# A 7x7 depthwise convolution cut image by image into tiles of six by four pixels, with each projection behind its own image's attention

## The chip, the core and the metric

The kernel runs on one core of a Trainium2 chip. The number that counts is the device time of one execution in microseconds: the median of three runs, which is 3268.41 us for the kernel before (3267.57 to 3269.32). One more execution was taken with the hardware profiler on. All data is float32. A core has a matrix engine (PE, with its weight loads shown apart as PEld), a vector engine (DVE), a scalar engine (ACT), GpSimd (POOL), and the sync engine (SP), which here only issues transfers between device memory and on-chip memory.

## The reference

The input is four images of 256 channels by 64 x 64 pixels. Two residual layers follow one another; each one normalises its input over groups of 8 channels first.

```python
# layer 0: 8 heads of 32; keys and values from a 2x2 strided convolution (1024 of each per image)
x = x + softmax((q k + q pos) * scale) v
# layer 1: 4 areas of 16 rows per image, attention inside an area (1024 keys), 8 heads of 32
qkv = conv1x1(gn(x), w_qkv)
out = softmax(q k * scale) v                       # per area
out = out + depthwise_conv7x7(v_full, w_pe, b_pe)  # over the whole image, zero padding 3
x = x + conv1x1(out, w_proj)
```

The change is about the line with `depthwise_conv7x7`: each of the 256 channels of v, in each of the four images, is convolved with its own 7 x 7 taps, and the sum with the attention's output goes through the last 1 x 1 product (`w_proj`), called the projection below.

## The kernel before, in words

**Units and steps.** The whole program is one line of 128 units, written out by hand: 64 for layer 0 (A), 16 per image, then 64 for layer 1 (B), 16 per image. A unit is the attention of 512 queries and four heads over 1024 keys, in 8 steps of 128 keys. In each step `scores` makes four products q k (line 261, tile `s`), ACT takes their exponentials (line 265, tile `p`), `weighted` makes four products with v (line 272, tile `av`), and DVE adds up the exponentials for the divisors (line 797). Once a unit, `divisors` makes four products with ones (line 281).

**Side work.** Everything else is planned with `at(unit, step, what)` and woven into the steps. Products go into a queue of tasks (`task`, `soon_tasks`, `advance`): a step makes the next part of the first task (two or three parts if many wait), and all of them write one on-chip accumulator tile, `ps_side`, which exists once. The helper `product` (line 155) makes four matmuls of 32 output channels each. Side work is q, k and v of layer 0 (`q0ps`, `k0ps`, `v0ps`), v of layer 1 with its channels in rows (`vals_ps`), k and q of layer 1 (`k1ps`, `q1ps`), the convolution (`conv_ps`, line 732) and the projection (`ops`). The order of instructions on each engine is the order in which the Python code emits them; SP issues its transfers in that order too, and a transfer that waits holds up all later ones of SP.

**The convolution before.** `plan_values` writes v of all four images to one device array `vals` with rows of pixels outermost, and separately to `vala`, from which attention reads. When the last value of the last image is stored, `plan_conv` takes four channels at a time, for all four images together: 64 times it loads 126 partitions (42 rows of pixels, three times, each shifted by one pixel) for two halves of the image with six transfers, and for every second one three transfers of banded weights. A banded matrix product over rows does seven taps in one direction and three in the other at once, so three shifted products make the seven columns. That is 24 matmuls of 126 x 32 weights against 256 columns for each group of four channels. These run from unit 70.5, one group every 0.52 units, to about unit 104.

**The projection before.** Since the convolution of all images ends that late, the attention of images 0 to 2 is stored (`store_att`, array `attd`) and read back; projections of these images are planned from unit 105.3 on, one chunk of 512 pixels every 0.8 units (`late`, `spread`). Only image 3 projects straight behind its attention. For one chunk, `load_rest` loads the convolution (one transfer of 2 KB runs), `add_conv` adds it, the bias and the attention on DVE, and `project` makes 16 matmuls.

Of the kernel before, what the change touches and what calls it, by code (L numbers as in the profile page):

```python
# [33 lines left out]
BAND = HH // 2 + 2 * HALO  # L34
BROWS = 42
TC = 8
# [18 lines left out]
def direct_path(  # L55
# [31 lines left out]
    attd = [[dram.tile([P, CT, CH], FP, name=f"attd_{b}_{c}") for c in range(NCH)] for b in range(B - 1)]  # L87

    vals = dram.tile([HH + 2 * HALO + BROWS - BAND, C, B, XP], FP, name="vals")

    vala = [[dram.tile([4, HD, NH, 4, XP], FP, name=f"vala_{b}_{a}") for a in range(NAREA)] for b in range(B)]
    conv = dram.tile([C, B, N], FP, name="conv")

    bands = dram.tile([C // TC, 9, BROWS + HH // 2 - 1, TC], FP, name="bands")

# [368 lines left out]
    def plan_b(b, u):  # L464
# [13 lines left out]
        def make_k(a, qd, half):  # L478
# [3 lines left out]
            for t in range(CT):  # L482
# [7 lines left out]
            S.activation(  # L490
                k[:, qd, :].rearrange("p (j t i) -> p t j i", t=4, i=32)[:, 2 * half : 2 * half + 2],
                ps.rearrange("p (t j i) -> p t j i", t=2, i=32), AF.Identity, bias=bqkv_sb[:, 1, qd : qd + 1],
            )
# [3 lines left out]
        def load_v(a, half):  # L497
            vcs[a, half] = pool.tile([P, NH // 2, 4, XP], FP, tag="vc", name=f"vc_{b}_{a}_{half}", bufs=2)
            nc.sync.dma_start(
                vcs[a, half], vala[b][a][:, :, half * NH // 2 : (half + 1) * NH // 2].rearrange("t c h r x -> (t c) h r x")  # L500
            )

        def make_v(a, half):

            if half == 0:
                kvs["v"] = v_tile(("B", b, a))
            v, vc = kvs["v"], vcs.pop((a, half))
            V.transpose(
                out=v[:, :, half * P : (half + 1) * P].rearrange("p (r j) (h c) -> p h r j c", j=2, c=HD),
                in_=vc[:, :, :, HALO : HALO + WW].rearrange("p h r (j w) -> p h r j w", w=HD),  # L510
            )
            if half == 1:
                vs["B", b, a] = v
# [17 lines left out]
        for a in range(NAREA):  # L531
            g = u + 4 * a
            at(g - 6, 3, lambda a=a: load(a))
            for t in range(CT):
                at(g - 5, 2 + 3 * t, lambda a=a, t=t: norm(a, t))
            for n in range(4):
                at(g - 4, 1 + 4 * n, lambda a=a, n=n: task(2, make_k, a, n // 2, n % 2))
            for half in range(2):
                at(g - 3, 2 + 5 * half, lambda a=a, half=half: load_v(a, half))
                at(g - 2, 2 + 4 * half, lambda a=a, half=half: make_v(a, half))  # L540
# [5 lines left out]

        def store_att(c):
            nc.sync.dma_start(attd[b][c], atts.pop(("B", b, c)))
# [5 lines left out]
        def load_rest(c):  # L554
            cv = chunk_tile(f"cv_{b}_{c}")
            nc.sync.dma_start(cv, conv[:, b, c * CH : (c + 1) * CH].rearrange("(t p) n -> p t n", p=P))
            att = None
            if c == NCH - 1:
                load_residual(c)
            if b < B - 1:  # L560
                att = chunk_tile(f"at_{b}_{c}")
                nc.sync.dma_start(att, attd[b][c])
            rest[c] = cv, att

        def add_conv(c):
            cv, att = rest[c]
            if c < NCH - 1:
                load_residual(c)
            if att is None:
                att = atts["B", b, c]  # L570
            for t in range(CT):
                V.scalar_tensor_tensor(cv[:, t, :], cv[:, t, :], bpe_sb[:, t : t + 1], att[:, t, :], ALU.add, ALU.add)

        def project(c, to):
            cv, ps = rest[c][0], ps_side(f"ops_{b}_{c}_{to}")
# [7 lines left out]
            V.scalar_tensor_tensor(xm[:, to, :], ps, bproj_sb[:, to : to + 1], xm[:, to, :], ALU.add, ALU.add)  # L583
# [4 lines left out]

        for c in range(NCH):
            g, j = u + 2 * c + 3, 5  # L590
            if b < B - 1:
                at(g, j + 1, lambda c=c: store_att(c))
                g, j = 0, int(NKT * (late + spread * (b * NCH + c)))
            else:
                at(g, j, lambda c=c: add_conv(c))
                at(g, j + 2, lambda c=c: soon_tasks([(2, project, c, to) for to in range(CT)]))
                g, j = (g - 1, 5) if c < NCH - 1 else (g - 2, 2)
            at(g, j, lambda c=c: load_rest(c))
            if b < B - 1:
                at(g, j + 4, lambda c=c: add_conv(c))  # L600
                at(g, j + 6, lambda c=c: soon_tasks([(2, project, c, to) for to in range(CT)]))
# [13 lines left out]

    def plan_zeros(g):


        def zeros():
            zero = pool.tile([P, 8 * B * XP], FP, tag="rows", name="zero", bufs=2)  # L620
            V.memset(zero, 0.0)
            for lo, hi in ((0, 3), (67, 71), (71, 74)):
                nc.sync.dma_start(
                    vals[lo:hi].rearrange("r c b x -> (r c b x)").rearrange("(p n) -> p n", n=8 * B * XP),
                    zero[: (hi - lo) * C // 8],
                )
            flat = bands.rearrange("k x i c -> (k x i c)").rearrange("(p n) -> p n", p=P)
            nc.sync.dma_start(flat, zero[:, : flat.shape[1]])

        def taps():  # L630
            tap = pool.tile([NTAP, C], FP, tag="cout", name="tap", bufs=2)
            nc.sync.dma_start(tap, wpe.rearrange("c k -> k c"))
            for n in range(7):
                nc.sync.dma_start(
                    bands[:, :7, BAND - 1 - n, :].rearrange("k x c -> x k c"),
# [808 lines left out]
```

## Time and profile before

| | before |
|---|---|
| median of three runs | 3268.41 us (3267.57 to 3269.32) |
| the profiled execution: its own time, and its span | 3270.47 us, 3268.7 us |
| granted PE clock, mean | 0.997 |
| busy share PE / DVE / ACT / POOL | 98% / 76% / 77% / 15% |
| matmul records | 29730 |
| DMA packets, of them under 512 B | 319853, 182652 |
| mean DMA rate | 122 GB/s |

The span runs from the first to the last instruction of the profiled execution. Each matmul of this float32 program appears as two matmul records and two weight loads, so the 1536 matmuls of the convolution are 3072 records. "Busy" time of a group is the union of its records, which overlap, since four matmuls that use different quarters of the array run side by side. The chain that ended last is followed back from the last instruction; a stretch of it on one engine is the time in which that engine set the pace. A bracket with an arrow says what ended an idle time.

### The profile page before, as it was taken

The numbers are of one execution on the slowest core, as the hardware profiler recorded it, in microseconds if no ns is written. First come the engines' busy times: TensorE is split into PE (matmuls) and PEld (weight loads), VectorE is DVE, ScalarE is ACT, GpSimd is POOL, SyncE is SP. The second block draws the span as 40 slices with busy tenths as digits, with TensorE's granted clock in tenths as the row PEclk, the third lists the DMA queues.
The fourth block names the chain that finished last, engine by engine and source line by source line (L and its number), as shares of the span: only waits on it lengthen the run. The fifth ranks groups of instructions, "written<-read, shape, count | busy, mean of one in ns | idle before, by whom it ended". The sixth has DMA issues, their size and how long they took to land.

```text
span 3268.7 us, 72561 instructions
## 1 busy us (share of the span) xinstructions
PE 3218.2 (98%) x29730; PEld 961.1 (29%) x29730; DVE 2491.6 (76%) x2621; ACT 2525.6 (77%) x2993; POOL 487.2 (15%) x923
## 2 busy tenths in 40 slices
PE   7999999999999999999999999999999999999997
PEld 4233323333233322222222333333333322222221
DVE  3777897779877787778876767666776778888887
ACT  3888788887888888888887777777777787776765
POOL 0111121111211111111111111111111111111111
PEclk9999999999999999999999999999999999999999
DMA  5312212313322213553236667676766643445431
GB/s 179 80 64 73 77 66 90 100 59 116 100 69 84 65 63 91 148 138 113 82 120 158 162 151 178 159 174 141 180 171 153 172 142 123 166 147 172 155 121 57
DMA packets 319853, 397.27 MB, mean 122 GB/s; under 512 B 182652, under 2 KB 215708, under 8 KB 319192
## 3 DMA queue, kind: packets, MB, share of 16 engines
q1 hardware_dynamic: 291064, 356.06, 38.5%
q0 software_dynamic: 28448, 36.48, 4.2%
q8 instruction: 236, 3.87, 0.5%
q14 instruction: 105, 0.86, 0.1%
HBM read 285.98 MB, written 106.42 MB: 120 GB/s over the span
## 4 chain that ended last, share of the span: by engine, by line
PE 94%; DMA 2%; issue 1%; ACT 1%; DVE 1%; SPq 0%; POOL 0%; DVEq 0%; ACTq 0%; POOLq 0%
PE s L261 33%; PE av L272 29%; PE conv_ps L732 5%; PE den L281 4%; PE k0ps L155 3%; PE k1ps L155 3%; PE q1ps L155 3%; PE v0ps L155 3%; PE q0ps L155 3%; PE ops L155 3%; PE vals_ps L155 3%; ACT p L265 1%; DVE p L797 1%; DMA conv<-cout 0%; DMA rows<-vals 0%
## 5 line engine op out<-in xcount | busy, mean ns | idle before, releaser
L797 DVE TENSOR_TENSOR p<-p 128x1024 f32<-128x1024 f32 x1792 | 2113.3, 1219 | 623.1 <-ACT p L265 583.3
L265 ACT ACTIVATE p<-s 128x1024 f32<-128x1024 f32 x2048 | 2016.9, 1027 | 571.9 <-PE s L261 564.0
L261 PE MATMUL s<-q,k_A 32*128 32x512 f32 x4096 | 608.2, 640 | 1.4 <-ACT p L265 0.9
L261 PE MATMUL s<-q,k_B 32*128 32x512 f32 x4096 | 588.7, 640 | 1.1 <-ACT p L265 0.8
L272 PE MATMUL av<-p,v_A 128*32 128x512 f32 x4096 | 551.1, 603 | 0.0
L272 PE MATMUL av<-p,v_B 128*32 128x512 f32 x4096 | 546.0, 604 | 0.0
L308 POOL DMA_DIRECT2D rb<-recs x508 | 252.4, 502 | 454.1 <-DMA recs<-few 377.5
L306 POOL DMA_DIRECT2D recs<-few x127 | 70.2, 553 | 1423.2 <-DVE sums L305 1372.1
L261 PEld LDWEIGHTS s<-q,k_A 32*128 32x128 f32 x4096 | 176.3, 183 | 357.8 <-issue 273.3
L261 PEld LDWEIGHTS s<-q,k_B 32*128 32x128 f32 x4096 | 162.5, 182 | 363.3 <-issue 290.5
L272 PEld LDWEIGHTS av<-p,v_A 128*32 128x32 f32 x4096 | 89.4, 108 | 383.0 <-issue 335.0
L272 PEld LDWEIGHTS av<-p,v_B 128*32 128x32 f32 x4096 | 87.6, 108 | 378.8 <-issue 332.9
L732 PE MATMUL conv_ps<-rows,band 126*32 126x256 f32 x3072 | 195.1, 379 | 0.0
L732 PEld LDWEIGHTS conv_ps<-rows,band 126*32 126x32 f32 x3072 | 123.0, 139 | 113.0 <-issue 78.3
L297 POOL DMA_DIRECT2D rows<-den_sb x127 | 74.6, 587 | 433.3 <-ACT den_sb L290 424.1
L281 PE MATMUL den<-p,ones 128*32 128x512 f32 x1024 | 137.8, 605 | 0.4 <-DVE p L797 0.4
L155 PE MATMUL ops<-cv,wp_sb 128*32 128x512 f32 x1024 | 129.8, 600 | 6.0 <-issue 6.0
L155 PE MATMUL vals_ps<-hv,wqkv_sb 128*32 128x512 f32 x1024 | 130.1, 596 | 3.9 <-ACT vout L669 3.8
L155 PE MATMUL k0ps<-taps,wk_sb 128*32 128x256 f32 x2048 | 130.6, 383 | 3.0 <-ACT taps L243 3.0
L155 PE MATMUL k1ps<-h,wqkv_sb 128*32 128x512 f32 x1024 | 128.7, 593 | 2.4 <-ACT cout L739 1.6
L155 PE MATMUL q0ps<-hq,wq_sb 128*32 128x512 f32 x1024 | 129.8, 592 | 0.0
L155 PE MATMUL q1ps<-h,wqkv_sb 128*32 128x512 f32 x1024 | 129.7, 596 | 0.1
(87 smaller groups left out, 1594.9 us busy)
## 6 DMA issues: line engine op xcount, KB each, us to landing
rb<-recs POOLq DMA_DIRECT2D x508, 64.0 KB, 2.4
rows<-vals SPq DMA_DIRECT2D x128, 189.0 KB
rows<-vals SPq DMA_DIRECT2D x128, 188.8 KB
rows<-vals SPq DMA_DIRECT2D x128, 188.7 KB
vala<-vout SPq DMA_DIRECT2D x128, 144.0 KB
vals<-vout SPq DMA_DIRECT2D x256, 72.0 KB
vc<-vala SPq DMA_DIRECT2D x32, 576.0 KB
hq<-in_x SPq DMA_DIRECT2D x32, 512.0 KB
```

The source lines that it names most:

```text
L155: T.matmul(out[cols, :], lhsT=lhsT[:, cols], rhs=rhs, start=start, stop=stop)
L261: T.matmul(pairs[h // 2][:, h % 2, :], lhsT=k[rows, unit[0], j * P : (j + 1) * P], rhs=q[rows, :], start=True, stop=True,)
L265: exps = [lambda i=i: S.activation(p[i], pairs[i], AF.Exp, scale=SCALE) for i in range(2)]
L272: T.matmul(av[HD * h : HD * h + HD, :], lhsT=v[:, j, unit[0] * P + HD * h : unit[0] * P + HD * h + HD], rhs=p[h // 2][:, h % 2, :], start= ...
L281: T.matmul(dens[g][HD * h : HD * h + HD, :], lhsT=ones, rhs=p[h // 2][:, h % 2, :], start=True, stop=True,)
L297: G.dma_start(rows, den_sb[0:P:HD, :])
L306: G.dma_start(recs.rearrange("h (q n) -> (h q) n", n=CH // HD), few[:, 1, :])
L308: G.dma_start(rb[HD * h : HD * h + HD, :], recs[h : h + 1, :].to_broadcast([HD, CH]))
L732: T.matmul(ps[HD * m : HD * m + HD, i], lhsT=band_tiles[k][:, g, :, part + c], rhs=xs[:, m % 2, c, :, 3 * g : 3 * g + WW], start=(g == 0), ...
L797: soon(1, lambda i=i: V.tensor_add(ps[0][i], ps[0][i], ps[j][i]))
```

## The change

Six rows by four columns of output pixels become one tile. With its halo a tile reads 12 x 10 pixels = 120 contraction rows, and one matrix of 120 x 32 (24 pixels and 8 rows of nothing needed) makes all 49 taps in one product. An image has 11 x 16 such tiles, which are the 176 columns of the product. A channel of an image then takes one matmul.

- `plan_values`: v is stored with the four columns of a tile apart (`vals[b]`, one array per image; runs of 18 numbers), in four transfers per half chunk where there were eight per chunk; the halves get tiles of their own (`vout`, which share five buffers, tag `vc`, with the tiles that attention reads).
- `plan_zeros`: the 120 x 32 matrices are put together once, early (`matrices`, units 4 to 13.4: 16 times ten small loads and a store to `mats`).
- `plan_conv`, `load_rows`, `convolve`: per image and group of eight channels, four loads (`rows`), every second time one of matrices (`band`), eight matmuls, one copy out of `ps_side`, one store. This is 128 groups. The loads run three groups ahead.
- The times: values of images 0 to 3 start at units 17.8, 42, 54.5 and 67; convolutions at units 36, 58, 75.5 and 93.5, one group every 0.53 to 0.68 units.
- `store_att` and `attd` are gone: every image projects straight behind its attention, from `add_conv(c)` at unit u + 2c + 3 (u the image's first unit) on. Its convolution is loaded one unit before, with 16 transfers (8 rows of pixels, 2 halves of the channels) of 64-byte runs instead of one.
- Columns of a tile stand apart in `cv`, so `add_conv` and the last addition read or write with a stride (`by_column`); the keys of an area change their order to that of the values (`make_k` copies in two halves, `make_v` transposes in four parts of two heads).

The diff, cut to its core:

```diff
-BAND = HH // 2 + 2 * HALO
-BROWS = 42
-TC = 8
+TY, TX, NY, XT, NP, TC = 6, 4, 11, WW // 4 + 2, 120, 16
+BY, BX = 12 + 7, 10 + 3
...
-            S.activation(
-                k[:, qd, :].rearrange("p (j t i) -> p t j i", t=4, i=32)[:, 2 * half : 2 * half + 2],
-                ps.rearrange("p (t j i) -> p t j i", t=2, i=32), AF.Identity, bias=bqkv_sb[:, 1, qd : qd + 1],
-            )
+            for n in range(2):
+                S.activation(
+                    k[:, qd, :].rearrange("p (r g t f x) -> p t r g f x", r=4, g=2, t=4, f=2)[:, 2 * half + n],
+                    ps[:, n * 256 : (n + 1) * 256].rearrange("p (r x g f) -> p r g f x", r=4, g=2, f=2),
+                    AF.Identity, bias=bqkv_sb[:, 1, qd : qd + 1],
+                )
...
         def load_rest(c):
             cv = chunk_tile(f"cv_{b}_{c}")
-            nc.sync.dma_start(cv, conv[:, b, c * CH : (c + 1) * CH].rearrange("(t p) n -> p t n", p=P))
-            att = None
+            for y in range(c * RC, (c + 1) * RC):
+                n, r = y // TY, TY - 1 - y % TY
+                for t in range(CT):
+                    nc.sync.dma_start(
+                        cv[:, t, :].rearrange("p (f r x) -> p r f x", f=TX, r=RC)[:, y - c * RC],
+                        conv[b][t * P : (t + 1) * P, r * TX : (r + 1) * TX, n, :],
+                    )
...
         def add_conv(c):
-            cv, att = rest[c]
+            cv, att = rest[c], atts["B", b, c]
...
-                V.scalar_tensor_tensor(cv[:, t, :], cv[:, t, :], bpe_sb[:, t : t + 1], att[:, t, :], ALU.add, ALU.add)
+                V.scalar_tensor_tensor(
+                    by_column(cv[:, t, :]), by_column(cv[:, t, :]), bpe_sb[:, t : t + 1],
+                    att[:, t, :].rearrange("p (q f) -> p q f", f=TX), ALU.add, ALU.add,
+                )
...
         for c in range(NCH):
             g, j = u + 2 * c + 3, 5
-            if b < B - 1:
-                at(g, j + 1, lambda c=c: store_att(c))
-                g, j = 0, int(NKT * (late + spread * (b * NCH + c)))
...
+            at(*((g - 1, 5) if b < B - 1 or c < NCH - 1 else (g - 2, 2)), lambda c=c: load_rest(c))
+            at(g, j, lambda c=c: add_conv(c))
+            at(g, j + 2, lambda c=c: soon_tasks([(2, project, c, to) for to in range(CT)]))
...
+        def matrices(k):
+            band = pool.tile([NP, 8, TX * TC], FP, tag="band", name=f"made_{k}", bufs=2)
+            for dc in range(10):
+                p, step = (48 * (dc // 4) + dc % 4, 4) if dc < 8 else (12 * dc, 1)
+                nc.sync.dma_start(
+                    band[p : p + 11 * step + 1 : step],
...
+            nc.sync.dma_start(mats[k], band)
...
+            for f in range(TX):
+                at_row = ((f + 1) % TX) * XT + (f == TX - 1)
+                nc.sync.dma_start(
+                    vals[b][HALO + c * RC : HALO + (c + 1) * RC, f, t * P : (t + 1) * P, :].rearrange("r p x -> p r x"),
+                    out[:, :, at_row : at_row + XT],
+                )
...
-        def convolve():
-            xs, (k, part) = made.pop("x"), divmod(4 * n, TC)
-            ps = ps_side(f"conv_ps_{n}").rearrange("p (i b x) -> p i b x", i=2, b=B)
-            for i in range(2):
-                for g in range(3):
-                    for m in range(4):
-                        c = 2 * (m // 2) + i
-                        T.matmul(
-                            ps[HD * m : HD * m + HD, i], lhsT=band_tiles[k][:, g, :, part + c],
-                            rhs=xs[:, m % 2, c, :, 3 * g : 3 * g + WW], start=(g == 0), stop=(g == 2),
-                        )
-                    if (i, g) in ((0, 1), (1, 0)):
-                        yield
...
+    def load_rows(b, n):
...
+        xs = loaded[b, n] = pool.tile([NP, NY, 8, XT], FP, tag="rows", name=f"rows_{b}_{n}", bufs=3)
+        row, size = C * XT, 8 * XT
+        for a, f, fs in ((0, 0, 4), (1, 0, 4), (2, 0, 1), (2, 1, 1)):
+            p = 12 * (4 * a + f)
+            nc.sync.dma_start(
+                xs[p : p + 12 * fs].rearrange("p y c x -> p y (c x)")[:, :, : size - 2],
...
+    def convolve(b, n):
+        xs, (k, part) = loaded.pop((b, n)), divmod(n, TC // 8)
+        size = NY * WW // TX
+        ps = ps_side(f"conv_ps_{b}_{n}")[:, : 2 * size]
+        for i in range(2):
+            for m in range(4):
+                T.matmul(
+                    ps[HD * m : HD * m + HD, i * size : (i + 1) * size].rearrange("p (y x) -> p y x", y=NY),
+                    lhsT=ready[b, k].rearrange("p y (x c) -> p (y x) c", c=TC)[:, :, 8 * part + 4 * i + m],
+                    rhs=xs[:, :, 4 * i + m, : WW // TX], start=True, stop=True,
+                )
+        out = pool.tile([P, 2, size], FP, tag="cout", name=f"cout_{b}_{n}", bufs=2)
+        S.copy(out.rearrange("p i y -> p (i y)"), ps)
...
+        if n + 3 < C // 8:
+            load_rows(b, n + 3)
+        yield
...
-    begin, pace = 70.5, 0.52
-    late, spread = begin + pace * (C // 4) + 1.5, 0.8
...
-            plan_values(b, c, ends[b] + 1.8 + (14.5 if b == 1 else 0) + (3.4, 1.0, 1.6, 0.4)[b] * c)
-    for n in range(C // 4):
-        plan_conv(n, begin + pace * n)
+            plan_values(b, c, (17.8, 42, 54.5, 67)[b] + (2.0, 1.5, 1.3, 2.2)[b] * c)
+        for n in range(C // 8):
+            plan_conv(b, n, (36, 58, 75.5, 93.5)[b] + (0.68, 0.53, 0.55, 0.55)[b] * n)
```

## The prediction

> **What bounds the kernel now.** I read the page's busy shares and the chain that ended last first: they name the engine.
>
> ```profile
> PE 3218.2 (98%) x29730; PEld 961.1 (29%) x29730; DVE 2491.6 (76%) x2621; ACT 2525.6 (77%) x2993; POOL 487.2 (15%) x923
> ...
> PE 94%; DMA 2%; issue 1%; ACT 1%; DVE 1%; SPq 0%; POOL 0%; DVEq 0%; ACTq 0%; POOLq 0%
> PE s L261 33%; PE av L272 29%; PE conv_ps L732 5%; PE den L281 4%; PE k0ps L155 3%; PE k1ps L155 3%; PE q1ps L155 3%; PE v0ps L155 3%; PE q0ps L155 3%; PE ops L155 3%; PE vals_ps L155 3%; ACT p L265 1%; DVE p L797 1%; DMA conv<-cout 0%; DMA rows<-vals 0%
> ```
>
> PE sets the pace for 94% of the span, the convolution for 5% of it, 163 us. A busy PE need not be a bound PE, so I next read the chain in order of time inside one unit of the convolution's stage (start, us, what), and two whole units as windows (PE busy with its records, then PEld, DVE, ACT, POOL): unit 47, with no side work, and unit 82, with much.
>
> ```profile
> 2074.60 1.07 PE s L261 x8
> 2075.67 1.00 PE av L272 x8
> 2076.67 0.87 PE conv_ps L732 x16
> ...
> 2082.53 1.72 PE k1ps L155 x16
> ```
>
> ```profile
> 1202.68:1221.25 18.57, 18.57 (x140) 4.88 (x142) 15.58 (x15) 16.67 (x19) 2.52 (x5) 1.00 0.25 77
> 2072.94:2099.88 26.94, 26.94 (x300) 10.16 (x296) 19.46 (x19) 19.11 (x23) 3.69 (x7) 1.00 0.81 221
> ```
>
> These are the prices. A step costs PE 1.07 + 1.00 = 2.07 us, a unit 8 x 2.07 = 16.5. A block of side work (four matmuls of 512 columns, 8 records) adds 0.86; 16 convolution records of 256 columns add 0.87, so 0.054 a record, 0.108 a matmul, and the time follows the columns. Unit 82 by this sum: 16.5, 3.5 blocks (one of divisors, two of k, half of q) 3.0, 68 convolution matmuls 7.3: 26.8, measured 26.94. Unit 47: 16.5 + 0.86 = 17.4, but it took 18.6. With little side work exponentials and sums are late too (DVE adds seven times two of 1219 ns, 17.1 us), and a unit doesn't go below some 18.5 to 20 us.
>
> I did this sum for all 127 units up to 3220.8 us, counting the matmuls of each from the order of PE's instructions. For sixteen units at a time: sum / time in windows:
> 0-15: 359.9 / 366.9; 16-31: 374.5 / 385.1; 32-47: 374.3 / 383.1; 48-63: 367.4 / 384.2; 64-79: 402.9 / 413.0; 80-95: 413.2 / 415.8; 96-111: 400.9 / 402.1; 112-126: 383.4 / 384.4.
> In all 3076.5 of 3134.6. The 58 us left over lie in empty units (1, 15, 17, 31, 47: two to three each), and at units 50 (7) and 66 (6), where the values of images 2 and 3 are normalised just as their statistics come: ACT waits for POOL, which stands before a small transfer of the divisors. From unit 80 on almost nothing is left over: there a matmul less is time less. Before unit 0 lie 86.2 us, after unit 126 lie 47.9.
>
> **What the Trainium skill says.** "TensorE: Matmul & The Clock Gate", Back-to-back issue gap, gives N / 2.4 + 2.5 ns for a matmul of N columns. Twice that per four side by side is 431 ns at 512 columns (here 0.86 / 2 = 430) and 218 at 256 (here 217): the trace agrees. The same page, LDWEIGHTS: time goes with the columns of the weights, 27 ns for 32. Here it is more, as the group of the convolution's loads shows: 123.0 / 3072 = 40 ns.
>
> ```profile
> L732 PE MATMUL conv_ps<-rows,band 126*32 126x256 f32 x3072 | 195.1, 379 | 0.0
> L732 PEld LDWEIGHTS conv_ps<-rows,band 126*32 126x32 f32 x3072 | 123.0, 139 | 113.0 <-issue 78.3 <-ACT cout L739 4.4 <-ACT q L527 0.9
> ```
>
> "DMA: Bandwidth & Descriptors", Specifications: under 512 B a transfer has to read, modify and write. The page has 182652 such packets of 319853 already; what they cost I bound below. "SBUF — State Buffer", section Door 1, says that fp32 accesses more than 16 bytes apart pay a penalty, of no stated size; no DVE row here has such a stride.
>
> **The change part by part.** *Convolution, PE.* Removed: 1536 matmuls x 0.108 = 165.9. Added: 1024 of 176 columns. By columns alone 0.074; the page's gap gives 2 x (176 / 2.4 + 2.5) = 152 ns per four records, but four weight loads at 40 ns are 160: 0.080 a matmul, 81.9 us. Low end 0.074 (75.8), high end the old 0.108 (110.6), since weights now stand 64 bytes apart instead of 32. I take 0.080: 84.0 us less on PE (55 to 90).
>
> *Moved PE work.* With the new order the same count per sixteen units gives 359.9, 384.8, 386.9, 367.1, 397.1, 387.2, 377.6, 331.8: 2992.4. Products are neither added nor dropped elsewhere. What was empty in 31, 46 and 47 is now filled with values and convolutions; units 115, 119, 123 and 125 become thin (18 to 20). Left over I put: 7 as before; 8 (unit 31 filled); 4; 9 (unit 50's wait goes, as values start at 54.5; ACT is busier); 9 (unit 66's goes, values start at 67; 5 for late transfers); 6; 5; 8 for the thin units: 56. In the tail 3 for 16 transfers in front of the last `xm` load.
>
> *ACT.* `cout` 128 x some 0.45 instead of 64 x 0.587 (20 us more), k in two halves (17 more). A unit of B has ACT at 21 of 24 us: hidden under PE; PSUM is now read with a stride, doubled that is 0.7 us more a copy, still under.
>
> *DVE.* `add_conv` and `xm`, 745 and 749 ns, become strided: between that and double, 3 us a chunk, 1.5 a unit. Units of B have 20 us of DVE, so 22 under 24; only units 112 to 126 (22.1 a unit on PE) would feel it, some 10 us. I take no penalty. `vout`'s memsets wait for stores five tiles back, over two units: hidden.
>
> *DMA.* SP's transfers in the built order rise from 1410 to 2151; in units 66 to 84 from 20 to 26 a unit, 85 to 110 from 16 to 20. SP issues at 0.4 to 0.84 us each, the worst being stores of values (two stretches of SP's order of time: start, us, how many):
>
> ```profile
> 1703.72 7.53 SPq L682 DMA_DIRECT2D vals<-vout  x8
> ```
>
> ```profile
> 2077.61 3.48 SPq L705 DMA_DIRECT2D rows<-vals  x6
> ```
>
> So 26 x 0.7 = 18 of 24.5 us: it fits, and the 16 loads of `cv` (10 us) have a unit of lead. New waits on SP: each store of `conv` waits for its copy on ACT and the next `load_rows` for its eight matmuls, 1 to 3 us, with `cv`, `xm` and stores of values queued behind; DVE waits for those. Packets: 256 stores x 1024 runs of 72 B and 512 loads x 512 runs of 64 B are new, loads of rows are 169,000 runs of 568 B. The nearest row is the wait for `tap<-in_wpe`, 12,544 single numbers in 18.9 us: even spread on all 16 engines at most 24 ns each. 524,000 at 24 ns are 0.8 ms of an engine's time, 24% of the span beside 43% now, less what goes. High end: the mean of now, 38.5% x 16 x 3268.7 / 291064 = 69 ns; then the queues would be full. The matrices (176 transfers in units 4 to 13, DMA at a quarter there) and the removed `attd` are hidden both ways.
>
> Sum: 86.2 + 2992.4 + 56 + 47.9 + 3 = 3185 us for the span, against 3268.7 for the profiled one, whose own time is 3270.47; the median of the runs, 3268.41, is the span within 0.3 us, so I take 3185 for it.
>
> **The rivals.** *Full price per matmul (0.15).* The short product costs as much as the long one because weight loads or strided reads set its pace: 110.6 instead of 81.9, and strided DVE work adds 10: 3224. For it: 139 ns a weight load here against 110 at the unstrided rows. Against: 256 columns follow the columns exactly.
>
> *Late transfers, moderate (0.12).* A step behind in units 66 to 84: `cv`, `xm` or memsets of `vout` come 3 us late for half of the 32 chunks, 50 us on DVE and through `p` on PE: 3235.
>
> *SP or the queues become the bound (0.12), slower than before.* In units 66 to 110 there are 19 x 26.1 + 26 x 20.3 = 1024 transfers beside some 1095 us of PE. Eight semaphores go round among them, so a transfer waits for the one eight back. At a price of 1.15 us each they eat the gain (1178 - 1095 = 83). If runs of 64 and 72 bytes take the 69 ns of the mean packet, 1.3 us each is near: 1331 - 1095, 236 more, 3421. For it: stores of 288-byte runs already take 0.94 us. Against: units 67 to 70 issue 26 to 32 transfers each, and PE's sum holds there within 1 us.
>
> *The change gives little (0.03).* Ends of work move, but the new thin units and ACT take it all back: 3268. Against it speaks the leftover near nothing after unit 80.
>
> **How the numbers follow.** Forecast 0.58 at 3185, own range 3155 to 3212; the rivals 0.15 at 3224, 0.12 at 3235, 0.12 above 3268, 0.03 at 3268. The range 3150 to 3262 leaves out SP's case and little more. Faster by over 0.2% (about what a measurement here can tell from none) 0.85, within 0.2% 0.03, slower 0.12.
>
> **What would show it.** Right: `conv_ps` at 2048 records and about 80 us of the chain (163 before); PE still above 90% of it; units 80 to 111 at 24 us, 112 to 126 at 22 to 23; no wait of 4 us or more at units 50 and 66. Price per matmul: mean time of `conv_ps` weight loads well over 139 ns, chain over 100 us. SP: waits of DVE for `cv<-conv`, `xm<-xmid` or `vals<-vout` of tens of us, DMA slices of 8 and 9 in units 66 to 84. Wrong altogether: PE's share of the chain falling below 85%, or strided `add_conv` at 1.5 us and over.

## The result: slower, and where the time went

The changed kernel takes 3397.56 us (median of four runs, 3392.82 to 3398.47) beside 3268.51 us of the kernel before on the same chip: a ratio of 1.039, interval 1.0374 to 1.041. The forecast was 3185. The profiled execution has a span of 3396.8 us, 128 more than before and 212 more than forecast.

The page of the changed kernel, busy shares and the chain that ended last (by engine, by line), as shown above for the kernel before:

```profile
PE 3194.6 (94%) x28706; PEld 929.2 (27%) x28706; DVE 2511.2 (74%) x2717; ACT 2543.9 (75%) x3121; POOL 488.7 (14%) x923
...
PE 44%; DMA 8%; SPq 4%; issue 4%; ACT 1%; DVE 1%; POOL 0%; ACTq 0%; DVEq 0%; POOLq 0%
PE s L263 16%; PE av L274 14%; PE q1ps L157 3%; PE ops L157 3%; PE k1ps L157 3%; SPq L698 2%; DMA vals<-vout 2%; PE den L283 2%; DMA hv<-xmid 2%; PE conv_ps L740 1%; DMA rows<-vals 1%; PE vals_ps L157 1%; DMA recs<-few 1%; SPq L558 1%; ACT p L267 1%
```

The chain could be followed through only part of the span, so its shares are no sums here (those of the engines add up to 62%); but transfers stand in it that weren't named before, `vals<-vout`, its issue on line 698 and `hv<-xmid`, each with 2%, and `rows<-vals` has grown from 0% to 1%. PE is busy for less of the span, though its work is the same by count as forecast.

The product itself did what the forecast said. The group of the convolution's matmuls and of its weight loads (after the bar busy us and mean ns of one, then the idle time before it):

```profile
L740 PE MATMUL conv_ps<-rows,band 120*32 120x176 f32 x2048 | 105.9, 322 | 37.5 <-DMA rows<-vals 18.1 <-ACT q L427 14.2 <-ACT k_B L493 3.5
L740 PEld LDWEIGHTS conv_ps<-rows,band 120*32 120x32 f32 x2048 | 80.6, 141 | 115.4 <-issue 80.2 <-ACT q L427 16.0 <-ACT cout L746 6.0
```

A weight load takes 141 ns, as before (139), though the weights are now 64 bytes apart. Where the time went shows in the windows of sixteen units each, for units 64 to 79, 96 to 111 and 112 to 126 (PE busy with its records, PEld, DVE, ACT, POOL; then clock, DMA share, GB/s):

```profile
1724.50:2215.00 490.50, 424.80 (x3584) 118.37 (x3580) 314.22 (x351) 328.10 (x405) 61.15 (x115) 0.92 0.84 144
...
2628.90:3008.70 379.80, 379.26 (x3380) 106.75 (x3376) 312.44 (x320) 307.20 (x373) 58.90 (x112) 1.00 0.71 142
3008.70:3348.60 339.90, 338.23 (x2706) 84.06 (x2700) 289.69 (x297) 272.10 (x312) 54.71 (x104) 1.00 0.30 66
```

From unit 96 on the forecast holds: 377.6 + 5 were foretold for the first of these stretches and 331.8 + 8 for the last, 379.8 and 339.9 came. Units 64 to 79 should have taken 397.1 + 9 and took 490.5. Against the sum of PE's work that the prediction gives, the eight stretches leave 7.0, 40.7, 18.9, 72.1, 93.4, 26.8, 2.1 and 8.2 us over: 269, where 56 were forecast. Nearly all of the excess of 213 us lies in units 20 to 82, which is where values are stored: beside the kernel with long runs that is shown below, no unit outside them is longer by more than 1.2 us.

The worst single unit is 64, with 51.9 us. SP's order of time in it (start, us it was held, line, transfer, how many):

```profile
1729.85 0.37 SPq L667 DMA_DIRECT2D hv<-xmid  x1
1730.80 0.38 SPq L747 DMA_DIRECT2D conv<-cout  x1
...
1739.58 8.67 SPq L698 DMA_DIRECT2D vals<-vout  x4
1748.37 1.51 SPq L690 DMA_DIRECT2D vala<-vout  x2
1749.93 8.12 SPq L698 DMA_DIRECT2D vals<-vout  x4
1758.15 0.73 SPq L747 DMA_DIRECT2D conv<-cout  x1
```

and the chain in order of time there (start, us, what):

```profile
1729.85 8.16 DMA hv<-xmid
...
1749.93 2.47 SPq L698
1752.45 0.96 SPq L698
1753.45 3.97 SPq L698
...
1758.15 7.43 DMA conv<-cout
1765.68 0.46 ACT cout L746
```

A store of values holds SP here for more than 2 us in the mean, four of them for over 8, and the store of a convolution behind them starts late and lands 7.4 us later; ACT can't write the next `cout` until then, and PE waits for `ps_side`. Over the whole run a store of values holds SP for 1.84 us in the mean (0.73 before) and its median time from issue to completion is 9.8 us (5.1 before). What was late shows in the waits of the changed kernel (engine, what waited for which transfer: us in total, times, longest):

```profile
ACT hv L245 <- DMA hv<-xmid: 101.8, 17, 14.2
...
DVE att_A L313 <- DMA rb<-recs: 75.3, 18, 9.1
...
ACT cout L746 <- DMA conv<-cout: 51.0, 7, 14.0
...
DVE st_A L338 <- DMA xs<-in_x: 36.0, 6, 8.4
```

Two readings of this stay possible: that SP is held too long (issue), or that the transfers themselves are slow (completion). The experiments part them.

### The profile page after: what moved, and what is told of

Same layout as the page of the kernel before. It is cut to its first block, busy times and chain, and to the rows that moved or that the text cites. A ratio compares the mean times of both kernels' runs of the same rounds, so it can differ in the third digit from the quotient of the medians.

```text
span 3396.8 us, 71851 instructions
## 1 busy us (share of the span) xinstructions
PE 3194.6 (94%) x28706; PEld 929.2 (27%) x28706; DVE 2511.2 (74%) x2717; ACT 2543.9 (75%) x3121; POOL 488.7 (14%) x923
## 4 chain that ended last, share of the span: by engine, by line
PE 44%; DMA 8%; SPq 4%; issue 4%; ACT 1%; DVE 1%; POOL 0%; ACTq 0%; DVEq 0%; POOLq 0%
PE s L263 16%; PE av L274 14%; PE q1ps L157 3%; PE ops L157 3%; PE k1ps L157 3%; SPq L698 2%; DMA vals<-vout 2%; PE den L283 2%; DMA hv<-xmid 2%; PE conv_ps L740 1%; DMA rows<-vals 1%; PE vals_ps L157 1%; DMA recs<-few 1%; SPq L558 1%; ACT p L267 1%
## 5 line engine op out<-in xcount | busy, mean ns | idle before, releaser
L263 PE MATMUL s<-q,k_A 32*128 32x512 f32 x4096 | 620.0, 650 | 29.6 <-ACT p L267 29.6
L263 PE MATMUL s<-q,k_B 32*128 32x512 f32 x4096 | 604.2, 647 | 23.8 <-ACT p L267 23.8
L274 PE MATMUL av<-p,v_A 128*32 128x512 f32 x4096 | 560.0, 612 | 0.0
L310 POOL DMA_DIRECT2D rb<-recs x508 | 252.0, 501 | 560.8 <-DMA recs<-few 465.0
L157 PE MATMUL ops<-cv,wp_sb 128*32 128x512 f32 x1024 | 139.0, 624 | 27.0 <-ACT vout L685 10.4
L283 PE MATMUL den<-p,ones 128*32 128x512 f32 x1024 | 145.0, 621 | 10.1 <-DVE p L802 10.1
L300 POOL DMA_DIRECT2D few<-rows x127 | 72.3, 569 | 520.0 <-DMA rows<-den_sb 514.8
L740 PE MATMUL conv_ps<-rows,band 120*32 120x176 f32 x2048 | 105.9, 322 | 37.5 <-DMA rows<-vals 18.1
L157 PE MATMUL v0ps<-wv_sb,taps 128*32 128x256 f32 x2048 | 127.9, 383 | 5.8 <-ACT cout L746 3.6
L245 ACT ACTIVATE hv<-hv,norm_B 128x512 f32<-128x512 f32 x64 | 52.5, 820 | 106.9 <-DMA hv<-xmid 101.8
```

The costliest lines, as they stand in the source:

```text
L157: T.matmul(out[cols, :], lhsT=lhsT[:, cols], rhs=rhs, start=start, stop=stop)
L263: T.matmul(pairs[h // 2][:, h % 2, :], lhsT=k[rows, unit[0], j * P : (j + 1) * P], rhs=q[rows, :], start=True, stop=True,)
L274: T.matmul(av[HD * h : HD * h + HD, :], lhsT=v[:, j, unit[0] * P + HD * h : unit[0] * P + HD * h + HD], rhs=p[h // 2][:, h % 2, :], start= ...
L283: T.matmul(dens[g][HD * h : HD * h + HD, :], lhsT=ones, rhs=p[h // 2][:, h % 2, :], start=True, stop=True,)
L300: G.dma_start(few[:, 0, :], rows.rearrange("h (q n) -> (h q) n", n=CH // HD))
L310: G.dma_start(rb[HD * h : HD * h + HD, :], recs[h : h + 1, :].to_broadcast([HD, CH]))
```

## The experiments

Each kernel below is the changed one with the edit shown, unless another kernel is named as its base, and the ratio is to the kernel before, measured beside it. "Landing" is the completion of a transfer.

**The stores in long runs.** The same 256 transfers and bytes, but 256 runs of 288 bytes in each instead of 1024 of 72. The pixels lie in another order, so other numbers are convolved.

```diff
+            long = vals[b].rearrange("r f c x -> r (f c x)").rearrange("r (c y) -> r c y", y=TX * XT)
...
-                    vals[b][HALO + c * RC : HALO + (c + 1) * RC, f, t * P : (t + 1) * P, :].rearrange("r p x -> p r x"),
-                    out[:, :, at_row : at_row + XT],
+                    long[lo : lo + 2, t * P : (t + 1) * P, :].rearrange("r p y -> p r y"), out[:, 2 * f : 2 * f + 2, :]
```

> The changed kernel, but each of the 256 stores of values writes two rows of all four columns in runs of 288 bytes instead of eight rows of one column in runs of 72 bytes: the same number of transfers and bytes, a quarter of the runs. The pixels then lie in another order than the convolution takes them to lie, so this kernel convolves other numbers; all else is unchanged. Theory A (the number of short runs fills the transfer queues and holds SP, and what stands behind comes late): a store takes SP about 0.75 us instead of 1.84, the waits for hv<-xmid go, the time falls to 3190 to 3220 us. Rival B (the number of transfers in SP's one queue, whatever their runs): no change, 3380 to 3400 us. Rival C (the loads of rows, 169,000 runs of 568 bytes, fill the queues): little change, above 3330 us.

It took 3190.93 us, ratio 0.976 (0.9733 to 0.9789), six microseconds from the forecast. The chain on its page, by engine:

```profile
PE 93%; DMA 2%; issue 2%; ACT 1%; DVE 1%; SPq 1%; POOL 0%; DVEq 0%; ACTq 0%; POOLq 0%
```

Its window of units 64 to 79, in the columns of the windows above:

```profile
1613.60:2021.50 407.90, 402.02 (x3584) 114.84 (x3580) 315.45 (x355) 327.09 (x404) 61.16 (x116) 1.00 0.79 166
```

PE is back at 93% of the chain, the stretch takes 407.9 (406 forecast), and a store holds SP for 0.68 us and lands after 5.1. So nearly the whole loss (207 of 213 us) hangs on the runs of the value stores; the new product, the 512 loads of `cv` in runs of 64 bytes (0.63 us on SP, 2.2 us to completion) and the strided reads cost nothing that shows.

**The late load earlier.** `hv`, the longest wait, loaded thirteen steps ahead instead of five.

```diff
-        at(0, when, load)
+        at(0, when - 8, load)
```

> The changed kernel with the load of hv planned 13 steps before its first use instead of 5. Theory A says what is late is whatever stands on SP behind value stores; of the excess over the sum of PE's work (213 us) the waits of ACT for hv<-xmid are 102 us: if these are the main way in which lateness reaches PE, 3290 to 3310 us. Rival D (each wait removed is replaced by the next late transfer, conv stores, rows, residuals): 3350 to 3395 us.

3407.4 us, ratio 1.042 (1.0393 to 1.0453). The waits of this kernel:

```profile
DVE att_A L313 <- DMA rb<-recs: 145.0, 27, 10.3
...
ACT cout L746 <- DMA conv<-cout: 81.7, 10, 21.3
...
DVE xm L590 <- DMA xm<-xmid: 56.8, 6, 15.9
```

The wait for `hv` is gone and these three together grew by more than it was (by 135 us; the last stood at 22.6). The late load was one of several victims, not the cause.

**The stores from another engine.** GpSimd issues them instead of SP.

```diff
-                nc.sync.dma_start(
+                nc.gpsimd.dma_start(
                     vals[b][HALO + c * RC : HALO + (c + 1) * RC, f, t * P : (t + 1) * P, :].rearrange("r p x -> p r x"),
```

> The changed kernel with the 256 stores of values issued from GpSimd's queue instead of SP's; data and runs are the same. If the cause is only SP's order (what stands behind a store on SP waits until SP is through with it), hv, rows and residuals come in time and the time falls to 3190 to 3240 us. If the cause is the work of the DMA engines on 262,144 short runs, or GpSimd itself is held long by writing descriptors and the divisors' small transfers behind it come late, it stays above 3330 us or rises.

3489.12 us, ratio 1.067 (1.0642 to 1.0704): worse still. SP is free of the stores, but GpSimd's own small transfers, which carry the divisors, now stand behind them, and a store lands after 12.9 us. The waits of this kernel:

```profile
POOL rb L310 <- DMA recs<-few: 584.3, 116, 16.9
...
DVE att_A L313 <- DMA rb<-recs: 169.1, 25, 21.6
...
DVE few L306 <- DMA few<-rows: 128.4, 21, 21.6
```

In the changed kernel they are 465.0, 75.3 and 26.7 us. GpSimd's queue has taken the place of SP's, so this run alone doesn't part the two readings.

**The burst pulled apart.** The two halves of a chunk's values five steps apart; alone, and with the early `hv`.

```diff
-            at(0, when + 7, lambda t=t: task(2, values, t))
+            at(0, when + 7 + 5 * t, lambda t=t: task(2, values, t))
```

> The changed kernel with the two halves of a chunk's values five steps (about 14 us) apart, so that SP is held twice by four stores (7.5 us each) with room between them instead of once by eight (17 us). Theory I, the loss comes from the burst: small transfers behind it are late by half as much and part of that hides in the room that they have: 3290 to 3350. Theory J, the loss follows the total work of the stores, wherever they stand: 3380 to 3420.

> Both: the halves five steps apart and the chunk for the values loaded thirteen steps ahead instead of five. Theory I: 3270 to 3340, below the run with the halves apart alone, since the early load no longer meets a burst of its own chunk. Theory J: 3380 to 3420, as each alone.

3412.26 (ratio 1.0445, 1.0427 to 1.0462) and 3379.95 (1.0338, 1.0321 to 1.0355). The first speaks for J, the loss follows the total; the second lies just under J's range and far above I's, a gain of 18 us on the changed kernel. Spacing cures next to nothing.

**Length of the runs.** Pairs of them, 512 runs of 144 bytes in a transfer.

```diff
+            pairs = vals[b].rearrange("r f c x -> r (f c x)").rearrange("r (g c y) -> r g c y", g=2, y=2 * XT)
...
+                    pairs[lo : lo + 4, g, t * P : (t + 1) * P, :].rearrange("r p y -> p r y"),
+                    out[:, 4 * (f // 2) : 4 * (f // 2) + 4, 2 * g * XT : 2 * (g + 1) * XT],
```

> Stores of values in runs of 144 bytes (512 in a transfer), with as many transfers and bytes as the changed kernel and as the kernel with runs of 288 bytes; the pixels lie in another order in the array, so other numbers are convolved, by the same instructions. Theory A, every run costs alike: SP holds a store (1.84 - 0.68) / 768 = 1.5 ns per run more, so 0.68 + 256 x 0.0015 = 1.07 us, and the time is a third of the way from 3190.9 to 3397.6: 3260, at least 3235. Theory F, the loss is a queue that is full beyond a point: SP holds about 0.75 us and the time is 3190 to 3215. Theory G, a cost of writes below 128 bytes or so rather than of the number of runs: SP holds 0.7 us, time 3190 to 3200. F and G differ in the landing: over 6.5 us by F, 5 us by G.

3205.52 us (0.9806, 0.979 to 0.9822). SP is held for 1.05 us, as A said (1.07), a store lands after 7.0, as F said, and the time is F's, not A's 3260. So SP is held longer by more runs, but that isn't what the time follows.

**Place of the runs.** As many runs as in the changed kernel, each 64 bytes on a multiple of 64.

```diff
+            even = vals[b].rearrange("r f c x -> r (f c x)")[:, : TX * C * 16].rearrange("r (f c x) -> r f c x", f=TX, x=16)
...
-                    vals[b][HALO + c * RC : HALO + (c + 1) * RC, f, t * P : (t + 1) * P, :].rearrange("r p x -> p r x"),
-                    out[:, :, at_row : at_row + XT],
+                    even[HALO + c * RC : HALO + (c + 1) * RC, f, t * P : (t + 1) * P, :].rearrange("r p x -> p r x"),
+                    out[:, :, at_row : at_row + 16],
```

> As many runs in as many transfers as the changed kernel, but each run is 16 of the 18 numbers, 64 bytes on a multiple of 64 bytes (72-byte runs begin on a multiple of 8 and touch two or three such pieces). Two of 18 numbers are left out and the rest lies in another place, so other numbers are convolved; the part of the array that stays empty is written early with zeros by 16 more transfers. Theory A, the number of runs counts: SP holds 1.7 to 1.9 us a store and the time is 3370 to 3410. Theory H, it is the runs' place and partial pieces: SP holds less than 1.2 us and the time is 3190 to 3280.

3210.25 us (0.982, 0.9803 to 0.9836). A's part on SP came nearly true, 1.49 us a store, and its time did not; H's time came true, and its part on SP did not. (A run of 72 bytes on a multiple of 8 always touches two pieces of 64, never three.) This parts the two readings. Unit 64 in SP's order of time:

```profile
1622.91 8.18 SPq L702 DMA_DIRECT2D vals<-vout  x4
1631.21 1.78 SPq L693 DMA_DIRECT2D vala<-vout  x2
1633.03 4.65 SPq L702 DMA_DIRECT2D vals<-vout  x4
1637.78 0.55 SPq L751 DMA_DIRECT2D conv<-cout  x1
```

The first four stores hold SP for 8.18 us here as well (the next four for 4.65 instead of 8.12), and the unit takes 27.4 us instead of 51.9: a held SP was nearly harmless. Over the whole run the 256 stores hold it for 206 us more than with long runs, and the time is 19 us longer. What changed against the changed kernel is that a store lands after 5.5 us instead of 9.8, and the others' waits fall with it:

```profile
ACT hv L245 <- DMA hv<-xmid: 11.7, 4, 3.6
ACT cout L750 <- DMA conv<-cout: 11.3, 3, 6.7
```

**Which places are dear.** Four kernels move or shorten the runs: the changed one with 72 bytes on multiples of 128, and three edits of the kernel with 64-byte runs: only 60 bytes of each; the runs moved as a whole by 32 bytes; and by 16. The numbers convolved are others in each; the gaps are filled with zeros by early transfers, which stand in units 2 to 14. In units 0 to 15 the first two take 8 and 18 us longer than with long runs, the price of the filling. In units 16 to 31, where the first values are stored, they take another 10 and 23 us longer.

```diff
-    vals = [dram.tile([TY * NY + 2 * HALO, TX, C, XT], FP, name=f"vals_{b}") for b in range(B)]
+    vals = [dram.tile([TY * NY + 2 * HALO, TX, C, 32], FP, name=f"vals_{b}") for b in range(B)]
...
-                    vals[b][HALO + c * RC : HALO + (c + 1) * RC, f, t * P : (t + 1) * P, :].rearrange("r p x -> p r x"),
+                    vals[b][HALO + c * RC : HALO + (c + 1) * RC, f, t * P : (t + 1) * P, :XT].rearrange("r p x -> p r x"),
...
-        row, size = C * XT, 8 * XT
+        row, size = C * 32, 8 * XT
```

> The changed kernel's stores of values as they are, 1024 runs of 72 bytes in a transfer, but the runs begin 128 bytes apart on multiples of 128, so that no two runs touch the same 64 bytes; each still ends with 8 bytes of a second piece. The rows are loaded in runs of the same length from the same array, which now holds other numbers there, so other numbers are convolved; 64 more transfers (4.7 MB an image) fill the gaps with zeros early, hidden or some 10 us. Theory K, what costs is that two runs share a piece of 64 bytes: SP holds a store for 0.7 us, time 3190 to 3235. Theory L, what costs is every piece of 64 bytes that is written in part: SP holds 1.5 us or more, 3330 to 3410.

```diff
-                    even[HALO + c * RC : HALO + (c + 1) * RC, f, t * P : (t + 1) * P, :].rearrange("r p x -> p r x"),
-                    out[:, :, at_row : at_row + 16],
+                    even[HALO + c * RC : HALO + (c + 1) * RC, f, t * P : (t + 1) * P, :15].rearrange("r p x -> p r x"),
+                    out[:, :, at_row : at_row + 15],
```

> The kernel with runs of 64 bytes on multiples of 64, but only 15 of 18 numbers, 60 bytes, are written of each: every run now writes its piece of 64 bytes in part, and no piece is touched by two runs. Three of 18 numbers are left out and other numbers are convolved; 128 more transfers (4.2 MB an image) fill the gaps with zeros early. Theory L, a piece written in part costs: landing above 7 us instead of 5.5, 3270 to 3310, as with 72 bytes 128 bytes apart (3289). Theory N, it was the second piece of each run that cost there, and a part of one does not: landing 5 to 6 us, 3205 to 3230.

```diff
-            even = vals[b].rearrange("r f c x -> r (f c x)")[:, : TX * C * 16].rearrange("r (f c x) -> r f c x", f=TX, x=16)
+            even = vals[b].rearrange("r f c x -> r (f c x)")[:, 8 : 8 + TX * C * 16].rearrange("r (f c x) -> r f c x", f=TX, x=16)
```

> The kernel with runs of 64 bytes on multiples of 64, moved by 32 bytes as a whole: as long, as many, side by side without gaps, but each run now writes two halves of two pieces, each shared with its neighbour. Other numbers are convolved. Theory L: two parts a run, at least the 1.75 of the changed kernel: landing 9 us or more and 3370 to 3420. Theory K or N: two pieces, shared: also slow, 3350 to 3420. A rival, P, that only the length of 72 bytes counts (or that what counts is a place off 32 bytes): 3205 to 3230.

The fourth kernel has the same line with 4 in place of 8.

> As the kernel with 64-byte runs moved by 32 bytes, but moved by 16: the same length and number of runs, side by side, each now writing 16 + 32 + 16 bytes of three pieces of 32, two of them in part and shared with a neighbour. Other numbers are convolved. Theory Q, pieces of 32 bytes written in part cost (1.5 of them a run in the changed kernel, 1 in the runs of 60 bytes and of 72 bytes 128 apart, a half as many in all with runs of 144, none with 288 and 64): landing 9 us or more, 3370 to 3450. Theory R, only a length that is no multiple of 32 bytes costs: landing 5.5 to 6 us, 3205 to 3230.

Measured: 3289.1 (ratio 1.0066, 1.0049 to 1.0083), 3335.1 (1.0206, 1.0189 to 1.0223), 3218.68 (0.9841, 0.9824 to 0.9857) and 3563.39 (1.0909, 1.089 to 1.0927). The first lies between K's range and L's, with SP held as L said (1.63 us). The second lies above both ranges, and its stores land after 8.0 us, as L said. The third was a miss for L, K and N alike and fell into P's range: 64-byte runs that cross from one piece of 64 bytes into the next are cheap when they begin on a multiple of 32. Moved by 16 bytes instead, the same runs are the dearest of all, above even Q's range; this and the 60 bytes refute P's first half, that only a length of 72 counts, while its second, a place off 32 bytes, stands. The chains of the kernels moved by 32 and by 16 bytes, by engine:

```profile
PE 90%; DMA 3%; issue 2%; ACT 2%; DVE 1%; SPq 1%; POOL 0%; DVEq 0%; ACTq 0%; POOLq 0%
PE 36%; DMA 9%; SPq 7%; issue 2%; ACT 1%; DVE 0%; POOL 0%; ACTq 0%; DVEq 0%; POOLq 0%
```

and the longest waits of ACT and DVE for transfers in the latter (13.9 and 24.4 us in the former):

```profile
ACT hv L245 <- DMA hv<-xmid: 192.8, 21, 23.6
...
DVE att_A L313 <- DMA rb<-recs: 119.5, 21, 12.2
```

All eight in one table. A run of 72 bytes begins at 0, 8, 16 or 24 past a multiple of 32 by turns and so writes 1, 2, 2 or 1 pieces of 32 bytes in part, 1.5 in the mean; one of 144 bytes always leaves one in part. Left over is the time of units 32 to 95 less the prediction's sum of PE's work there (1538.3 us), which keeps the early filling out. It comes from the profiled execution, as do the two columns before it; the last column is the median, from which that execution differs by up to 9 us (longer in the second and third row, shorter in the last).

| runs of a store | pieces of 32 bytes in part, a store | SP held, us | issue to completion, us | left over, us | time, us |
|---|---|---|---|---|---|
| 256 x 288 | 0 | 0.68 | 5.1 | 33 | 3190.9 |
| 1024 x 64 on 64 | 0 | 1.49 | 5.5 | 63 | 3210.3 |
| 1024 x 64, moved by 32 | 0 | 1.47 | 5.9 | 68 | 3218.7 |
| 512 x 144 | 512 | 1.05 | 7.0 | 50 | 3205.5 |
| 1024 x 72 on 128 | 1024 | 1.63 | 7.6 | 113 | 3289.1 |
| 1024 x 60 on 64 | 1024 | 1.69 | 8.0 | 134 | 3335.1 |
| 1024 x 72 (the change) | 1536 | 1.84 | 9.8 | 211 | 3397.6 |
| 1024 x 64, moved by 16 | 2048 | 2.25 | 11.8 | 331 | 3563.4 |

Four times as many runs cost 19 us of time and 30 us of what is left over (first row to the second); the rest goes with the pieces written in part, little at first and 80 to 120 us of what is left over for every 512 more at the end. The count isn't all: the two rows with 1024 differ by 21 us. Between the third row and the last nothing differs but the place, for length and number are equal and the runs lie side by side in both: 345 us. A write of part of a piece that makes the memory read it first would be a reason, and the Trainium skill names one like it ("Collectives: The Full Stack", Rules for kernel authors, asks for buffers of collectives to be aligned to 32 bytes since that prevents a read-modify-write by the hardware). These runs agree with the 32 bytes and don't show the mechanism.

**A version of the whole computation with 64-byte stores.** No column of zeros is stored with a row, so a row of 16 numbers is 64 bytes; the first or last column of the shifted rows is zeroed on chip.

```diff
-TY, TX, NY, XT, NP, TC = 6, 4, 11, WW // 4 + 2, 120, 16
+TY, TX, NY, XT, NP, TC = 6, 4, 11, WW // 4, 120, 16
...
-                at_row = ((f + 1) % TX) * XT + (f == TX - 1)
...
-                    out[:, :, at_row : at_row + XT],
+                    out[:, :, f * XT : (f + 1) * XT],
...
+    def edges(b, n):
+        xs = loaded[b, n]
+        V.memset(xs[0:36, :, :, 0], 0.0)
+        V.memset(xs[64:100, :, :, XT - 1], 0.0)
...
+        if n + 1 < C // 8:
+            edges(b, n + 1)
```

> A version that computes the whole reference with values stored in runs of 16 numbers, 64 bytes on a multiple of 64: no column of zeros is stored with a row; instead the first or last column of the shifted rows is set to zero on chip by two small DVE instructions per group (256 instead of the 128 before), and rows are loaded with eight transfers of 512-byte runs instead of four of 568. Both K and L expect stores of 0.7 us on SP. 512 more loads on SP at 0.4 us are 200 us of SP, which has room: 3195 to 3225. A rival, M: the number of transfers on SP does decide once there are 2660 of them, and they come late by turns: 3240 to 3300.

3224.99 us, ratio 0.986 (0.9844 to 0.9877): faster than both kernels, and 1.4% below the one before, at the upper end of what was expected. A store holds SP for 1.29 us, not for 0.7. Rival M falls: 2723 transfers stand in SP's queue, more than in the changed kernel (2147), and hold it for 1520 us in all instead of 1662. It stays 15 us above the run with 64-byte stores of other numbers. DVE waited 35 us for rows before the new instructions; two edits of this version aim at that, the first with these instructions one step before the product and an image's first rows loaded earlier, the second with the earlier load alone.

```diff
-        if n + 1 < C // 8:
-            edges(b, n + 1)
...
-            at(0, when - 6, lambda: load_rows(b, n))
+            at(0, when - 10, lambda: load_rows(b, n))
...
+        at(0, when - 1, lambda: edges(b, n))
```

> The version with 64-byte stores and zeroed edges that computes the whole reference, with the two small DVE instructions of a group one step ahead of its product instead of a whole group ahead, and the first rows of an image loaded ten steps ahead instead of six. DVE waited 35 us for rows there, eight times. If these waits pass to PE: 3195 to 3220; if others take their place: 3220 to 3230, as before.

```diff
-            at(0, when - 6, lambda: load_rows(b, n))
+            at(0, when - 10, lambda: load_rows(b, n))
```

> The version with 64-byte stores and zeroed edges that computes the whole reference, its DVE instructions a group ahead as at first, with only the first rows of an image loaded ten steps ahead instead of six. If DVE's 35 us of waits for rows stand at the first groups and pass to PE: 3200 to 3218; if they stand elsewhere: 3219 to 3229, as before.

3268.76 (ratio 0.9994, 0.9987 to 1.0001) and 3225.98 (0.9873, 0.9857 to 0.989). The first made it worse beyond both of its expectations. Its waits:

```profile
DVE rows L742 <- DMA rows<-vals: 114.7, 21, 15.4
```

A likely reason, which no run tests: products run behind the planned time when the queue of tasks is long, and their loads with them; an instruction that follows the planned time then stands on DVE just behind its load, and the sums of all exponentials wait after it. Bound to the product before, as at first, it has a group's time of room. The second changes nothing, as its second expectation said (DVE waits 40.0 us for rows, in eight waits as before); where the 15 us are stays open.

## Why the prediction was wrong

- **The price of the product** (0.080 us a matmul, 84.0 us less on PE) was right as far as the runs show: weight loads take 141 ns (139 before), the kernel with long runs takes 3190.93 us against 3185, and in its chain `conv_ps` stands for 2.3% of the span, some 73 us (163 before, 80 foretold). The rival with the full price per matmul, over 100 us, falls.
- **Moved PE work and what is left over** were right once the stores have long runs: 60 us over in that kernel, 56 forecast. The filled units 46 and 47 leave nothing over.
- **ACT and DVE** were right in effect. `cout` takes 458 ns (0.45), k in two halves 473. Strided `add_conv` takes longer, 1138 ns for 745, where none was taken:

```profile
L575 DVE SCALAR_TENSOR_TENSOR cv<-cv,bpe_sb,att_B 128x512 f32<-128x512 f32 x64 | 69.8, 1138 | 0.0
```

  That is 64 x 0.39 = 25 us of DVE, and units 112 to 126 still took the forecast time (339.9 us for 339.8). `xm`, with as wide a stride on the accumulator, kept its 747 ns.
- **The DMA step failed**, where it says "it fits". In the sum the wrong term is what is left over, 56 us put and 269 measured. Two things under it were wrong. The price of a store of values on SP, 0.4 to 0.84 us (the line shown there gives 7.53 / 8 = 0.94), was read from stores of 288-byte runs and kept for 72-byte ones: measured 1.84. By itself this would have cost little, as the aligned runs show, with 1.49 us a store. The other is the loss: the step put no price on how long a store takes to complete and on what that does to the transfers around it, and took the only wait for stores that it names, that of the memsets of `vout`, as hidden. A store completes after 9.8 us in the median, 5.1 before. The estimate per packet was not at fault in the mean (24 ns at most; the records of the 72-byte packets have a mean of 18.0 and a median of 12). What it left out is a tail: 3048 of 262144 of them last over 200 ns, against 27 of 525072 packets of 64 bytes in the aligned kernel, 101 in the one moved by 32 bytes and 4899 in the one moved by 16.
- **The quoted page** ("DMA: Bandwidth & Descriptors", Specifications: below 512 bytes a transfer reads, modifies and writes) led astray: it made the stores of before, 288 bytes, look like the same case. Here runs of 288 and of 64 bytes that fill pieces of 32 are cheap, and runs of 60, 64 and 72 bytes that don't are dear, so 512 bytes is not the line between them. No run stores values in runs of 512 bytes or more, so a smaller cost of all shorter ones is not ruled out.
- **The rival "SP or the queues become the bound"** was nearest, 3421, but its number came near by luck. Its point of decision was a mean of 1.15 us for each transfer of units 66 to 110; SP is held there for 0.66 us in the mean (0.77 over the whole run). Loads in 64-byte runs, half of its case, cost nothing that shows. And about two thirds of the loss lie before unit 66. Slower than before was given a chance of 0.12.
- **What would show it**: PE's share below 85% of the chain came true (44%, and 71% of the part that could be followed), and so did "late transfers", at four times the size put on it. The signs of SP's case came true in part and mislead: DMA slices of 8 stand in units 66 to 84, but also in the kernel with long runs, which loses nothing (0.84 and 0.79 in units 64 to 79); DVE waits 22.6 us for `xm<-xmid`, 14.3 for `vals<-vout` and not at all for `cv<-conv`, while the longest waits stand elsewhere, as shown above for `hv`.

## What to carry to other kernels

Before a layout makes the runs of a store shorter, work out where each begins and ends in memory: here runs that begin and end on multiples of 32 bytes were worth 345 us at the same length and number, while four times as many whole runs cost 19. A price read from stores that fill such pieces doesn't hold for stores that don't. When a wait disappears and the time doesn't fall, ask what made the transfer slow, not how to start it earlier.

## What the runs showed of the hardware beyond that

- The cost falls on others too: packets of 4096 bytes, which no store of values uses, last 253 ns in the mean in the changed kernel, 218 in the aligned one and 215 with long runs, by the packet records of the trace; in the kernel moved by 16 bytes 274, in the one moved by 32 219.
- A stall costs PE more than its length, by these figures: in units 64 to 79 PE is busy for 424.80 us in the changed kernel at a granted clock of 0.92, and for 402.02 us at 1.00 with long runs, for the same 3584 records: 23 of the stretch's 83 extra us.
- Reading in short runs need not be dear: 512 loads of 512 runs of 64 bytes complete in 2.2 us each. Their runs begin on multiples of 64 bytes; short reads that begin elsewhere were not tried.
